# Layer 1 of a two-layer kernel on one core: two batches' gates and shared expert products at a time, the time steps in a lane of their own, and two shared tiles

## Chip, core and metric

The kernel runs on one core of a Trainium2 chip. The metric is the device time of one execution in microseconds (us); it is given as the median of several runs. The engines are TensorE (PE in the profile; PEld is its weight load), VectorE (DVE), ScalarE (ACT), GpSimd (POOL) and SyncE (SP, which here only issues DMAs). Each engine works through its own queue of instructions in order; an instruction that waits holds up all that is queued behind it on the same engine.

## What is computed

The input is x of shape (4, 512, 256): four batches of 512 tokens. Two layers follow, each with a mixer and an expert block. Every block is applied to a layer norm of x, and the layer norm of its result is added to x:

```python
x = x + _layernorm(_L0_attn_ref(_layernorm(x), ...))   # Mamba-like mixer, 32 heads, and a dense feed-forward
x = x + _layernorm(_L0_ffn_ref(_layernorm(x), ...))    # 8 experts, top 2 per token
x = x + _layernorm(_L1_attn_ref(_layernorm(x), ...))   # diagonal state space mixer
x = x + _layernorm(_L1_ffn_ref(_layernorm(x), ...))    # 8 experts, top 2, and a shared expert
```

The change lies in layer 1. Cut to what matters, its two blocks are:

```python
projected = hidden @ in_proj_w.T                          # 256 -> 512 channels
X    = silu(causal_conv(projected))                       # 4 taps along the tokens
gate = sigmoid(hidden @ gate_proj_w.T)
dt   = softplus(einsum('blhp,hp->blh', X, dt_w) + dt_b)   # 8 heads of 64 channels: the time step
a, u = exp(dt * A), dt * B * X
s    = diag_ssm_scan(a, u)                                # s[t] = a[t] * s[t-1] + u[t]
out  = ((C * s + D * X) * gate) @ out_proj_w.T

scores = sigmoid(x @ gate.T)                              # the top 2 of 8 experts keep their score
routed = score of expert e times x                        # for each chosen expert e
out_r  = sum over e of (silu(routed @ w1[e].T) * (routed @ w3[e].T)) @ w2[e].T
out    = (silu(x @ shared_w1.T) * (x @ shared_w3.T)) @ shared_w2.T + out_r
```

## The kernel before

A batch of 512 tokens is the unit of work: x of each batch stays in SBUF as four chunks of 128 tokens, and most tiles are 128 partitions by 512 elements. The first part of the program, up to about 860 us, runs layer 0's mixer for the four batches, with the dense feed-forward of batches 0 to 2 and the routed experts of batches 0 and 1 squeezed in beside it. The second part, which the change touches, has what is left: the dense feed-forward of batch 3 (`last_feed_forward`), the routed experts of layer 0 for batches 2 and 3 (`experts0_in`, `experts0_out`, `experts0_back`), and all of layer 1 for the four batches.

The work of the second part is written as generators, one kind per stage, each run for the batches 0 to 3 in turn. A stage with its place in its list of batches is called a lane. Before the change there are eight lanes: 0 `last_feed_forward`, 1 to 3 the experts of layer 0, 4 `mixer1_in`, 5 `mixer1_out`, 6 `experts1_in`, 7 `experts1_out`. A stage yields after each step a tuple of estimated costs: time on TensorE, time on VectorE, a delay until the next step can start, and at times a fourth number, `need`. A planner at the end of `tile_layers` keeps an estimated clock for TensorE (`pe`) and VectorE (`dve`) and always takes the next step of the lane that is due and stands first in a fixed ranking (batches 2 and 3 before 0 and 1 for the lanes of layer 0 and the mixer). A lane is held back while its `need` names a lane that has not got far enough. The program is then scheduled on the engines' queues by the compiler, which may interleave neighbouring steps further; what counts is the order that comes out on each queue.

What the stages of layer 1 do, with the lines that the profile names:

- `mixer1_in`: layer norm of x (statistics L113 and L114, a power on POOL L123, scaled copies on ScalarE L148), transposes (L135) copied into `xT` by L137; four products with `w1i` (L1054), each followed by the convolution (L199 on ScalarE, three taps L201 on VectorE) and a Silu (L1058) into `X`, which has two buffers; four gate products with `w1g` (L1064) through Tanh (L1065) into `Gt`, one tile of 128 x 4 x 512 with one buffer; then the time steps: 16 small products with `dtw` (L1070), a bias (L1074), a softplus (L206 Abs, L209 Exp, L210 and L211, L212 Ln, L213, L1077). `by_row` turns the steps (L253), copies them (L255) into a tile tagged `row`, writes them to DRAM (L257).
- `mixer1_out`: the steps come back from DRAM, broadcast over 64 partitions (L1088), into `db`, one buffer. For each of four channel blocks: a product on POOL (L1092, `uu`), Exp and a scaled copy on ScalarE (L1093, L1094), on VectorE the scan (L1097), L1098 and the gate (L1099, in place in `Gt`), and four products with `w1o` (L1102). Then add_layernorm (L113, L114, L121, L123, L163, L172).
- `experts1_in`: layer norm, transposes, a bf16 cast (L1136, `xb`), router products (L245), Tanh (L1139), selection of the two experts by small VectorE instructions (L219 to L231, L1142 to L1146), and the shared expert's gated product (L1114, Silu L1116, L1117) into `hs`, one buffer.
- `experts1_out`: for each chunk of 128 tokens two halves of four experts: products (L1164), four Silus (L1169) into a tile tagged `s2b` (two buffers), four VectorE products (L1172) into `he`. For each two chunks: transposes (L1183), copies (L1186, L1188), products (L1194, L1196), add_layernorm, the last scaling on ScalarE (L174) and the store of the result (L1198).

Of the routed experts of layer 0, three lines matter here: the products of a tile of 128 rows (L459 and L467), the gathers of rows and weights by POOL (L441, L444), and, in `experts0_back`, the gathers of the results (L494), which are scaled on ScalarE (L498) and added on VectorE (L499).

ScalarE's functions need tables, and a change from one set to another shows in the profile as an ACT_TABLE_LOAD at the line of the function that needs it.

## Time and profile before

| what | us |
|---|---|
| median of 4 runs | 1298.07 |
| the four runs | 1298.01, 1302.82, 1298.08, 1298.06 |
| the profiled execution, its own time | 1303.1 |
| its span, first to last instruction | 1301.4 |
| PE busy | 1125.3 (86% of the span) |
| DVE busy | 794.5 (61%) |
| ACT busy | 545.1 (42%) |
| POOL busy | 325.0 (25%) |

The profile is of one execution. Its own time is 1.7 us longer than its span, and 5 us longer than the median of the four runs; its mean granted TensorE clock is 0.951. A timeline gives start, duration, engine, line and operation, then in square brackets how long the engine had been idle before and which instruction ended that. A view by stretches of time gives the busy time of each engine in each stretch with the number of its instructions, the granted TensorE clock (1.00 is full speed), the share of the DMA engines and the rate. A view by lines gives for each group of instructions the count, the busy time together, the mean duration in ns of one and the idle time before them. A product of 32-bit numbers shows as two records.

### The profile page before, as it was taken

What the parts mean: (1) busy time and instruction counts of PE and PEld (TensorE: products, weight loads), DVE (VectorE), ACT (ScalarE), POOL (GpSimd) and SP (SyncE); (2) the same over time, 40 slices, a digit from 0 to 9 for tenths busy, and PEclk for the clock granted to TensorE, in tenths of its full rate; (3) what the DMA queues carried; (4) which work ended last, traced back from release to release, by engine and by line L of the source; (5) the groups of instructions that cost most, each with busy time, mean ns of one, the idle gap of its engine ahead of it and who ended that gap; (6) DMA issues with size and microseconds to landing.
All of it is one profiled execution on the core that took longest, in us unless ns stands there. A gap on an engine that the chain in (4) does not pass through costs nothing. (4 is left out here: it accounts for less than half of the span.)

```text
span 1301.4 us, 18525 instructions
## 1 busy us (share of the span) xinstructions
PE 1125.3 (86%) x6896; PEld 698.1 (54%) x6896; DVE 794.5 (61%) x1742; ACT 545.1 (42%) x984; POOL 325.0 (25%) x411
## 2 busy tenths in 40 slices
PE   5688988999888999999989999988988696877876
PEld 3344545556545655555545665554666474454543
DVE  5567766656775564677774556754253554966765
ACT  2253442332434334332424443313154556786644
POOL 4021202001214432111133323123143833120100
PEclk9898999999898999999989999998999898999888
DMA  5010100011104453010114441125365552010100
GB/s 154 19 50 17 33 26 27 17 53 33 33 18 133 153 148 116 25 53 18 50 60 129 151 138 57 46 66 175 101 171 189 162 158 78 1 49 1 42 17 25
DMA packets 76153, 97.41 MB, mean 75 GB/s; under 512 B 11008, under 2 KB 62208, under 8 KB 76064
## 3 DMA queue, kind: packets, MB, share of 16 engines
q0 software_dynamic: 13488, 45.10, 11.8%
q1 hardware_dynamic: 53936, 43.26, 11.1%
q10 hardware_dynamic: 8640, 7.87, 1.8%
q8 instruction: 55, 0.90, 0.3%
q14 instruction: 34, 0.28, 0.1%
HBM read 85.25 MB, written 12.12 MB: 75 GB/s over the span
## 5 line engine op out<-in xcount | busy, mean ns | idle before, releaser
L540 PE MATMUL ps_pj<-uT,wg 128*128 128x512 f32 x512 | 262.2, 637 | 12.6 <-ACT bt L698 7.4
L201 DVE SCALAR_TENSOR_TENSOR BT<-ps_pj,col,BT 128x511 f32<-128x511 f32 (+2 forms) x192 | 143.4, 747 | 120.0 <-ACT BT L199 111.3
L719 POOL TENSOR_SCALAR_AFFINE_SELECT sc<-sc 128x1024 f32<-128x1024 f32 x64 | 69.9, 1092 | 476.0 <-DVE sc L716 468.6
L201 DVE SCALAR_TENSOR_TENSOR CT<-ps_pj,col,CT 128x511 f32<-128x511 f32 (+2 forms) x192 | 142.6, 743 | 21.1 <-ACT CT L199 18.3
L540 PEld LDWEIGHTS ps_pj<-uT,wg 128*128 128x128 f32 x512 | 92.4, 198 | 101.9 <-issue 74.6
L199 ACT ACTIVATE CT<-ps_pj,col 128x512 f32<-128x512 f32 x64 | 49.7, 777 | 119.4 <-PE ps_pj L540 119.4
L713 PE MATMUL ps_dc<-CT,BT 64*128 64x128 f32 x1024 | 89.4, 293 | 7.6 <-DVE sc L716 6.0
L713 PEld LDWEIGHTS ps_dc<-CT,BT 64*128 64x128 f32 x1024 | 70.7, 189 | 46.5 <-issue 29.4
L716 DVE TENSOR_TENSOR sc<-sc,ps_dc 128x1024 f32<-128x1024 f32 x64 | 77.7, 1214 | 23.7 <-PE ps_dc L713 21.2
L308 PE MATMUL ps_dc<-vT,wf 128*128 128x512 f32 x192 | 88.0, 597 | 1.9 <-issue 1.2
L199 ACT ACTIVATE BT<-ps_pj,col 128x512 f32<-128x512 f32 x64 | 49.7, 776 | 85.6 <-PE ps_pj L540 82.0
L708 ACT ACTIVATE sc<-ps_dc 128x1024 f32<-128x1024 f32 x64 | 65.6, 1025 | 40.0 <-PE ps_dc L705 37.6
L444 POOL DMA_INDIRECT wx<-in_w_exp_dram,wrow x60 | 59.2, 986 | 91.2 <-PE ps_dc L467 42.0
L467 PE MATMUL ps_dc<-wx,hx 128*128 128x256 f32 x240 | 65.9, 400 | 10.2 <-ACT h L498 4.7
L459 PEld LDWEIGHTS ps_dc<-hx,wx 128*128 128x128 f32 x480 | 60.9, 191 | 19.4 <-ACT hx L454 9.0
L459 PE MATMUL ps_dc<-hx,wx 128*128 128x128 f32 x480 | 65.1, 279 | 5.0 <-DMA wx<-in_w_exp_dram,wrow 3.0
L441 POOL DMA_INDIRECT xr<-XD,token x60 | 58.7, 979 | 42.2 <-PE ps_dc L452 26.4
L698 ACT COPY bt<-ps_pj 128x384 f32<-128x384 f32 x64 | 30.5, 476 | 82.3 <-PE ps_pj L696 73.3
L463 DVE TENSOR_TENSOR hx<-hx 128x256 f32<-128x256 f32 x60 | 27.5, 459 | 58.6 <-ACT hx L462 43.3
L467 PEld LDWEIGHTS ps_dc<-wx,hx 128*128 128x128 f32 x240 | 43.8, 194 | 29.4 <-issue 8.5
L308 PEld LDWEIGHTS ps_dc<-vT,wf 128*128 128x128 f32 x192 | 35.3, 190 | 42.0 <-issue 39.9
L730 PEld LDWEIGHTS ps_pj<-xd,bt 128*128 128x128 f32 x384 | 47.7, 196 | 16.5 <-issue 8.2
(315 smaller groups left out, 2016.4 us busy)
## 6 DMA issues: line engine op xcount, KB each, us to landing
wg<-in_w_in_dram SPq DMA_DIRECT2D x64, 256.0 KB
YS<-yr ACTq DMA_DIRECT2D x60, 128.0 KB
wf<-in_w_gate_dram SPq DMA_DIRECT2D x32, 128.0 KB
wf<-in_w_up_dram SPq DMA_DIRECT2D x32, 128.0 KB
wf<-in_w_down_dram SPq DMA_DIRECT2D x32, 128.0 KB
db<-dD SPq DMA_DIRECT2D x32, 128.0 KB
St<-Mv SPq DMA_DIRECT2D x192, 2.0 KB
x<-in_x_dram SPq DMA_DIRECT2D x4, 512.0 KB
```

The source lines that it names most:

```text
L199: S.activation(dst, p, AF.Identity, bias=bias, scale=w(3))
L201: V.scalar_tensor_tensor(dst[:, s:], p[:, : L - s], w(3 - s), dst[:, s:], ALU.mult, ALU.add)
L308: T.matmul(p, we[:, i * 2 + k, :], vT[:, k, :], start=(k == 0), stop=(k == 1))
L441: keep(G.indirect_dma_start(out=xr[t], out_offset=None, in_=x, in_offset=bass.IndirectOffsetOnAxis(ap=token[:, t : t + 1], axis=0)))
L444: keep(G.indirect_dma_start(out=ws[t], out_offset=None, in_=w_exp, in_offset=bass.IndirectOffsetOnAxis(ap=wrow[:, t : t + 1], axis=0)))
L459: T.matmul(p[:, L + d * P : L + (d + 1) * P], w[:, k * DM + d * P : k * DM + (d + 1) * P], h[:, k * P : (k + 1) * P], start=(k == 0), stop ...
L467: T.matmul(p[:, 2 * P : 2 * P + DM], h[:, (2 + d) * P : (3 + d) * P], w[:, (2 + d) * DM : (3 + d) * DM], start=(d == 0), stop=(d == 1))
L540: T.matmul(p, w[:, k, :], uT[:, k, :], start=(k == 0), stop=(k == 1))
L708: S.activation(sc, df, AF.Exp)
L713: T.matmul(cb[:, e * L + c * P : e * L + (c + 1) * P], of.BT[e * 64 : (e + 1) * 64, c * P : (c + 1) * P], of.CT[e * 64 : (e + 1) * 64, c * ...
L716: V.tensor_tensor(sc, sc, cb, ALU.mult)
L719: G.affine_select(out=scv, in_=scv, compare_op=ALU.is_ge, fill=0.0, base=0, pattern=[[0, 2 * NC], [1, P]], channel_multiplier=-1)
```

## The change

- `by_row` takes its tile for the turned steps from the tag `s2b`, which the experts' Silus use, with its two buffers; the tag `row` goes.
- The last feed-forward's input `vT` takes the tile `xTe` that `experts1_in` uses for its transposed input, in place of one of its own.
- The tag `hf`, three buffers of 128 x 512 for the last feed-forward's hidden values, gets eight buffers. The gates `Gt` become four tiles of this tag per batch, so that two batches' gates can be held. `hs` gets two buffers.
- `mixer1_in` ends after the gates; the time steps become a stage of their own, `mixer1_steps`, in a lane between `mixer1_in` and `mixer1_out`. There are nine lanes then: 5 is `mixer1_steps`, 6 `mixer1_out`, 7 `experts1_in`, 8 `experts1_out`.
- The planner's holds: before, the gates of batch b waited until `mixer1_out` of batch b - 1 was written out, and the shared product of batch b until `experts1_out` of b - 1 was. Now `X` and the gates of batch b wait for `mixer1_out` of batch b - 2, the gates for the last feed-forward too, and the shared product for `experts1_out` of batch b - 2.
- The planner's estimate for VectorE changes: a step's VectorE time is put after the running VectorE clock or 4 us before the TensorE clock, and no more after the step's own due time.

No arithmetic changes. Lines from L1066 on move by 2, 5 or 10: the gate products become L1066, the step products L1075, the output products L1107, the shared product L1119 and L1122, the expert products L1169, their Silus L1174.

```diff
@@ -251,7 +251,7 @@
         p = ps(bank, 2 if bank == "dc" else 1)
         for c in range(NC):
             T.transpose(p[:8, c * P : (c + 1) * P], wt[:, c, :], ident)
-        wT = wk.tile([8, L], F32, tag="row", name=tag, bufs=1)
+        wT = wk.tile([8, L], F32, tag="s2b", name=tag, bufs=2)
         S.copy(wT, p[:8, :L])
         d = dram.tile([8, L], F32, tag=tag, name=tag, bufs=2)
         nc.sync.dma_start(out=d, in_=wT)
@@ -986,7 +986,7 @@
         wes = [load(f) for f in range(2)]
         yield 0.0, 0.0, 0.0
         v = wl.tile([P, NC, DM], F32, tag="v", name="v", bufs=1)
-        vT = wk.tile([P, 2, L], F32, tag="vTf", name="vT", bufs=1)
+        vT = wk.tile([P, 2, L], F32, tag="xTe", name="vT", bufs=1)
         yield from normed(b, v, vT)
         acc = ps("o", 2)
         pend = []
@@ -1001,7 +1001,7 @@
                 for i, p in enumerate((gp, up)):
                     for k in range(2):
                         T.matmul(p, we[:, i * 2 + k, :], vT[:, k, :], start=(k == 0), stop=(k == 1))
-                h = wk.tile([P, L], F32, tag="hf", name="hf", bufs=3)
+                h = wk.tile([P, L], F32, tag="hf", name="hf", bufs=8)
                 S.activation(h, gp, AF.Tanh, scale=0.5)
                 V.scalar_tensor_tensor(h, h, 1.0, gp, ALU.add, ALU.mult)
                 V.scalar_tensor_tensor(h, h, 0.5, up, ALU.mult, ALU.mult)
@@ -1046,7 +1046,7 @@
         yield 0.0, 2.8, 4.0
         xT = wk.tile([P, 2, L], F32, tag="xTb", name="xT1", bufs=1)
         turned(xT, xn, "b")
-        yield 1.0, 0.0, 1.8
+        yield 1.0, 0.0, 1.8, 18
         t.X = X = wk.tile([P, 4, L], F32, tag="X", name="X", bufs=2)
         for m in range(4):
             p = ps("b")
@@ -1056,14 +1056,19 @@
                     later(i)
             conv(X[:, m, :], p, lambda t, m=m: cv("cw1", m * 4 + t), cv("cb1", m))
             S.activation(X[:, m, :], X[:, m, :], AF.Silu)
-            yield 1.72, 2.3, 0.0, (5 if m == 3 else 0)
-        t.Gt = Gt = wk.tile([P, 4, L], F32, tag="Gt", name="Gt", bufs=1)
+            yield 1.72, 2.3, 0.0, (19 if m == 3 else 0)
+        t.Gt = []
         for m in range(4):
+            g = wk.tile([P, L], F32, tag="hf", name="Gt", bufs=8)
+            t.Gt.append(g)
             p = ps("b")
             for k in range(2):
                 T.matmul(p, w1g[:, k, m * P : (m + 1) * P], xT[:, k, :], start=(k == 0), stop=(k == 1))
-            S.activation(Gt[:, m, :], p, AF.Tanh, scale=0.5)
+            S.activation(g, p, AF.Tanh, scale=0.5)
             yield 1.72, 0.0, 0.0
+
+    def mixer1_steps(b, t):
+        X = t.X
         dp = ps("b").rearrange("p (c a h) -> p c a h", a=16, h=8)
         for c in range(NC):
             for m in range(4):
@@ -1096,10 +1101,10 @@
                 yield 0.0, 0.0, 2.0
             V.tensor_tensor_scan(s, a[:, m, :], s, 0.0, ALU.mult, ALU.add)
             V.scalar_tensor_tensor(s, s, BC[:, m : m + 1], X[:, m, :], ALU.mult, ALU.add)
-            V.scalar_tensor_tensor(Gt[:, m, :], Gt[:, m, :], 1.0, s, ALU.add, ALU.mult)
+            V.scalar_tensor_tensor(Gt[m], Gt[m], 1.0, s, ALU.add, ALU.mult)
             yield 0.0, 2.8, 0.3
             for c in range(NC):
-                T.matmul(outs[:, c * DM : (c + 1) * DM], Gt[:, m, c * P : (c + 1) * P], w1o[:, m, :],
+                T.matmul(outs[:, c * DM : (c + 1) * DM], Gt[m][:, c * P : (c + 1) * P], w1o[:, m, :],
                          start=(m == 0 and c % 2 == 0), stop=(m == 3 and c % 2 == 1), skip_group_check=True)
             yield 1.72, 0.0, 0.0
         yield 0.0, 0.0, 0.5
@@ -1144,8 +1149,8 @@
         V.tensor_tensor(o1, o1, o2, ALU.add)
         t.s = small.tile([P, NC, 8], F32, tag="s1", name="s1")
         V.tensor_tensor(t.s, o1, sc, ALU.mult)
-        yield 1.8, 4.5, 0.5, 7
-        t.hs = wk.tile([P, L], F32, tag="hs", name="hs", bufs=1)
+        yield 1.8, 4.5, 0.5, 28
+        t.hs = wk.tile([P, L], F32, tag="hs", name="hs", bufs=2)
         gated(t.hs, sw1, sw3, xT)
         yield 3.44, 0.7, 0.5
 
@@ -1213,7 +1218,7 @@
     none = lambda b: iter(())
     stages = [lambda b: last if b == B - 1 else none(b)]
     stages += [lambda b, f=f: f(b, held1[b]) if b > 1 else none(b) for f in (experts0_in, experts0_out, experts0_back)]
-    stages += [lambda b, f=f: f(b, held1[b]) for f in (mixer1_in, mixer1_out, experts1_in, experts1_out)]
+    stages += [lambda b, f=f: f(b, held1[b]) for f in (mixer1_in, mixer1_steps, mixer1_out, experts1_in, experts1_out)]
     N = len(stages)
     rank = [2, 3, 0, 1]
     left = [[0.0] * N for _ in range(B)]
@@ -1223,11 +1228,15 @@
     while any(l[0] < B for l in lanes):
         ready = []
         for n, (b, gen, at, need) in enumerate(lanes):
-            if n == 5 and lanes[0][0] < B or need and lanes[need][0] < b:
+            if n == 6 and lanes[0][0] < B:
+                continue
+            if need in (18, 19) and lanes[6][0] < b - 1 or need == 19 and lanes[0][0] < B:
+                continue
+            if need == 28 and lanes[8][0] < b - 1:
                 continue
             if b < B and (gen or n == 0 or lanes[n - 1][0] > b):
                 at = at if gen or n == 0 else max(at if b == 0 else 0.0, left[b][n - 1])
-                first_of = min(rank[b:]) if n < 6 else rank[b]
+                first_of = min(rank[b:]) if n < 7 else rank[b]
                 ready.append((at, (first_of if n < 4 else 4 + first_of) + 0.1 * n, n))
         now = [r for r in ready if r[0] <= pe] or [min(ready)]
         at, _, n = min(now, key=lambda r: r[1])
@@ -1243,8 +1252,9 @@
             pe = max(pe, at) + step[0]
             at = pe
         if step[1]:
-            dve = max(dve, at - step[0]) + step[1]
-            at = max(at, dve if step[2] else dve - 4.0)
+            dve = max(dve, pe - 4.0) + step[1]
+            done = max(dve, at - step[0] + step[1])
+            at = max(at, done if step[2] else done - 4.0)
         l[2] = at + step[2]
         l[3] = step[3] if len(step) > 3 else 0
 
```

## Prediction

> **What bounds the kernel now.** I read the page first, then busy time by stretches of the tail, then VectorE's and TensorE's timelines there. The page: no engine is full, and the chain that ended last is spread thin over all of them, with no single line to remove.
>
> ```profile
> span 1301.4 us, 18525 instructions
> ...
> PE 1125.3 (86%) x6896; PEld 698.1 (54%) x6896; DVE 794.5 (61%) x1742; ACT 545.1 (42%) x984; POOL 325.0 (25%) x411
> ...
> DVE 5%; PE 4%; ACT 4%; issue 2%; POOL 2%; DMA 0%; POOLq 0%; ACTq 0%; SPq 0%; DVEq 0%
> ```
>
> The change touches layer 1 and the last feed-forward alone, so I went to the tail. The last product of layer 0's routed experts (L467, batch 3) starts at 1074.30 and takes 1.13, so it ends at T = 1075.4. After T only layer 1 is left. The stretches (columns as the first line says; counts in brackets) are cut at T and where VectorE starts four marked instructions.
>
> ```profile
> core 0: us, PE busy (x) PEld busy (x) DVE busy (x) ACT busy (x) POOL busy (x), PEclk, DMA share, GB/s
> 1002.00:1075.40 73.40, 57.02 (x283) 42.00 (x284) 38.77 (x97) 40.40 (x83) 41.77 (x38) 0.93 0.55 161
> 1075.40:1100.10 24.70, 15.72 (x85) 11.20 (x84) 8.90 (x32) 16.73 (x29) 10.14 (x10) 0.90 0.30 92
> 1100.10:1150.00 49.90, 40.02 (x182) 23.68 (x182) 39.38 (x115) 38.18 (x72) 7.49 (x7) 0.95 0.01 4
> 1150.00:1206.70 56.70, 45.94 (x198) 28.13 (x197) 39.53 (x107) 39.88 (x74) 9.83 (x7) 0.92 0.08 29
> 1206.70:1256.00 49.30, 38.47 (x208) 25.55 (x207) 37.15 (x114) 27.94 (x62) 8.47 (x8) 0.85 0.11 33
> 1256.00:1301.40 45.40, 31.21 (x166) 17.86 (x164) 24.90 (x100) 17.96 (x53) 2.79 (x4) 0.87 0.07 24
> 1075.40:1301.40 226.00, 171.36 (x833) 106.42 (x831) 149.86 (x463) 140.70 (x287) 38.72 (x36) 0.90 0.09 30
> ```
>
> The reader is to see that after T nobody is full: in 226.0 us TensorE is busy 171.4, VectorE 149.9, ScalarE 140.7. Time is lost in waits between them. The marks in VectorE's timeline are the shared expert's product of batch 0 (L1117) and the casts of batches 1 and 2 (L1136):
>
> ```profile
> 1100.11 0.67 DVE L1117 TENSOR_TENSOR hs<-sg,ps_dc 128x512 f32<-128x512 f32 x1
> ...
> 1150.00 0.69 DVE L1136 CAST xb<-xT 128x1024 bf16<-128x1024 f32 x1 [0.67 <-ACT xT L137]
> ...
> 1206.67 0.69 DVE L1136 CAST xb<-xT 128x1024 bf16<-128x1024 f32 x1 [1.18 <-ACT xT L137]
> ```
>
> TensorE's timeline shows the kind of loss (in brackets: idle before it, and who ended it). These are the three largest single waits after 1101; all its waits after T that the timeline lists add up to 40 us.
>
> ```profile
> 1202.90 1.02 PE L253 MATMUL ps_b<-ident,dts 128*8 128x128 f32 x4 [5.26 <-DVE dts L1077]
> ...
> 1220.18 1.06 PE L1183 MATMUL ps_b<-identb,he 128*128 128x128 bf16 x4 [5.39 <-DVE he L1172]
> ...
> 1250.77 1.95 PE L135 MATMUL ps_dc<-ident,xn 128*128 128x128 f32 x4 [3.00 <-ACT xn L148]
> ```
>
> The first is batch 3's time step: between the Exp and the Ln of its softplus ScalarE loaded tables four times in 5 us (loads of 1.28 at 1197.65, 1199.19, 1200.87, 1202.41), since the experts' Silu stood between. The other two wait for VectorE's expert product and for a layer norm, both queued in order with nothing else ready.
>
> **The change, part by part.** The instruction orders of the two compiled programs hold no times, but say what moves.
>
> *Moved across T.* The count of TensorE's instructions up to the last L467 is nearly the same in both programs, but ahead of T the changed one has also the last two gate products of batch 1 (4 records, 1.7 us from eight in 3.6), its time step product (L1070, 3.7), its transposes (L253, 0.4) and batch 2's input transposes (8 in 1.8): 7.5 us of TensorE. They go into the stretch 1002 to 1075.4, where TensorE's listed waits add up to 16.8 us (the largest, 4.75 before 1015.75, is for ScalarE's scaling of gathered rows). So they need not delay T, but from 1040 on TensorE is over 90% busy, so I let 2 us through: T becomes 1077.4. If nothing were absorbed it is 7.5; if the missing table loads (below) shorten the stretch, it is -3.
>
> *VectorE after T.* I add the rows' busy time per instruction over every VectorE instruction issued after that point (expert product 0.29, convolution tap 0.73, scan 1.27, add of a normed row 0.48, statistics 0.39 and 0.15, and so on). Before: 168.1. After: 171.0, as batch 0's add_layernorm and its next statistics come to stand behind T, and batch 1's first scans go ahead of it. Rows overlap, so 168.1 shows as 149.9 busy; I use the sums on both sides. Before, the five stretches hold 10.6, 43.9, 43.2, 41.4 and 29.0 in 24.7, 49.9, 56.7, 49.3 and 45.4 us: 0.43, 0.88, 0.76, 0.84 and 0.64 of the time. After, the sums are 38.7 up to batch 0's shared expert product, 38.3 up to batch 1's cast, 38.6 up to batch 2's shared product, and 55.4 to the end.
>
> *First stretch after.* In VectorE's new order batch 3's gathered rows, batch 2's convolution, batch 1's last scans and batch 3's norms all stand ahead of batch 2's time step. The gathers:
>
> ```profile
> 1081.09 1.02 POOL L494 DMA_INDIRECT h<-YS,place  x1 [8.91 <-issue]
> ...
> 1090.06 0.96 POOL L494 DMA_INDIRECT yg<-YS,place  x1 [0.30 <-issue]
> ```
>
> They start 5.7 after T and are 1.28 apart, and VectorE takes the last one 17.5 after T (L499 at 1092.88). In POOL's new order they stand behind batch 0's rsqrt and the last product `uu` of batch 1. Those need some 4.7 of VectorE's rows and 1.3 of POOL after T, about 6: hidden behind the 5.7; any delay beyond costs batch 3 one for one. Behind the last gather stand 6 taps (4.4), statistics (2.3), two scans and a product (3.3), a rsqrt on POOL with its hops (1.2), four adds (2.9), statistics (2.3) and three products (2.2): about T+37, with gaps T+38.5. Then the time step's chain: from its bias add to L253 took 7.7 (1080.75 to 1088.41) and 7.8 (1195.07 to 1202.90): T+46.2. On TensorE that wait (L253) now has batch 0's last router products (0.7), batch 3's transposes (1.8) and batch 0's shared expert (3.6) behind it, and then Silu 0.6: batch 0's shared product comes at T+53. TensorE has 33 us of work in it (16 records of L1054 and of L1064 at 0.45 each, 26 of L1102 at 0.22, and the above), so it idles about 20.
>
> TensorE's clock shows what such idling costs: after the 5.39 wait four transposes L1183 took 1.06, where eight usually take 0.61, and the granted clock is 0.85 and 0.87 in the last two stretches. I add nothing, since VectorE ends this stretch. The Trainium skill, "TensorE: Matmul & The Clock Gate", section "Why this matters for your kernels", speaks against this change: no gaps over about 3 us between bursts of matmuls, or the clock falls back to half. By its window of 3.4 us, three such gaps would cost an estimated 3 times 1.7 us, and the sum below would end 5 us later.
>
> *Next stretches.* Batch 2's scans, batch 3's convolution and batch 0's experts are all ready together, as between 1100 and 1150, with the same eleven table loads; at that stretch's 0.88, 38.3 take 43.5. The next 38.6 at the mean of the three middle stretches (128.5 in 155.9, 0.82) take 46.8. Bounds: 0.76 and 0.95.
>
> *Last stretch.* Three batches' experts follow each other, since all four mixers are now done first; batch 3's chain of norm, transposes and router (1238 to 1270 in the open before) is behind batch 1's and 2's products. The last batch alone takes 30.8 (first L1164 of batch 3 at 1270.60 to 1301.4) and holds 16.2 of the sum (32 products 9.3, two copies 1.4, two norms 5.5). The other 39.2 I take at 0.95: one table is loaded in it, against eleven in the stretch at 0.88. Bounds 0.76 and 1.12 (168.1 over 149.9, never waiting). 41.3 + 30.8 = 72.1.
>
> *Table loads.* 56 instead of 63 of ScalarE, five of the seven after T: 7 at 1.28 are 9.0 us of ScalarE. They are in the shares above; for themselves I count nothing, as ScalarE is busy 62% there. Between Exp and Ln of batch 3 no Silu stands any more: the 5.26 wait should be about 2.6 (two loads) shorter.
>
> *Shared tiles.* The row tile that by_row now takes from `s2b` holds one of the two Silu buffers until its DMA has read it. In the new order at least 4.5 us of ScalarE instructions lie between the copy and the next Silu that needs that buffer. The 16 KB store and the broadcast load after it took 7.5 together at worst without other cover (L253 1202.90 to POOL's product at 1210.39), so the store alone is below it: 0, at most 3 for each of batches 2 and 3. The feed-forward's input in `xTe` waits for nobody, since mixer1_out and so experts1_in came after the last feed-forward already. `hf` with 8 and `hs` with 2 buffers add no instruction. On SP's queue all loads of `db` now stand ahead of the output stores; with one buffer they wait, as before, for the last scan of the mixer before.
>
> *Sum.* T 1077.4 + 53 + 43.5 + 46.8 + 72.1 = 1292.8 against 1301.4, so 8.6 less. The profiled execution took 1303.1 (1.7 around its span), the median of the four runs is 1298.07: I take the difference off the median, **1289.5 us**.
>
> **Rivals.**
> 1. *Larger gain.* The new order lets VectorE keep 0.88 all the way to the last 14 us (after batch 3's last expert product, 1287.5, only a tail of 5 is left): (171.0 - 5) / 0.88 + 14 = 203, and T 1077.4: 1280, or with T unmoved 1278, so 21 to 23 less: 1276. For it: 0.88 was reached with eleven loads in it. Against: the first stretch is chained, as worked out.
> 2. *No difference.* The idle time moves: what the last stretch gains, the first one (20 us idle TensorE) gives back. With 0.76 in the two middle stretches they take 101.2 instead of 90.3, and the sum is 1303.7 on the span, or +2: 1300.
> 3. *Slower.* The mechanism is TensorE's queue ahead of T: batch 1's gates and steps stand between batch 3's routed experts, and if the 16.8 us of waits there stay where they are (they end with gathers and ScalarE's queue, which the change does not hurry) the 7.5 us are added to T. Then VectorE at its present mean (168.1 in 226.0, 0.744) takes 171.0 / 0.744 = 230, 4 more: +11, 1309. It decides where T slips by more than 5 and the mean share does not rise.
> 4. *It doesn't do what it says*: ruled out by the order; two batches' gates are issued before the first output product.
>
> **Numbers.** Forecast (its own range 1282 to 1294) 0.44; larger gain 0.16; no difference 0.17; slower 0.23. So faster by over 0.3% (3.9 us, about what a measurement of this kernel can tell from none) 0.60, within it 0.17, slower 0.23. The range reaches from past the larger gain, 1271, to the slower rival, 1309; the middle bound of 0.95 and T at -3 lie inside it.
>
> **What would show it.** T between 1074 and 1080. Batch 0's shared product on VectorE about 53 after T, with TensorE waiting there for the time step. The 5.26 wait at batch 3's L253 about halved. In the last 70 us three batches' L1164 in a row, no wait of 3 us for a layer norm between, VectorE busier than the 24.9 in 45.4 it has now. Wrong it would be if T slips by 6 or more, or if VectorE's share after T stays at 0.66 busy.

## The result, and the profile after

The changed kernel takes 1306.44 us (median of 48 runs, 1298.13 to 1316.69), the kernel before beside it 1300.36 (74 runs, 1294.64 to 1309.37): a ratio of 1.0041, 95% interval 1.0030 to 1.0051. It is slower by 0.4%, where 0.7% faster was forecast. The profiled execution took 1308.19, its span is 1306.5, its mean clock 0.948.

The lines of the page of after that answer to those of before:

```profile
span 1306.5 us, 18519 instructions
...
PE 1129.3 (86%) x6896; PEld 700.3 (54%) x6896; DVE 795.6 (61%) x1742; ACT 536.9 (41%) x977; POOL 322.0 (25%) x411
...
PE 3%; DVE 2%; ACT 1%; issue 0%; POOL 0%; POOLq 0%; ACTq 0%; DVEq 0%
```

Seven instructions of ScalarE are gone (984 to 977), as the orders said: the table loads. TensorE is busy 4 us longer for the same 6896 records.

T, the end of the last L467, is 1087.2 in place of 1075.4 (forecast 1077.4). Below are the stretches of after by time, the first ahead of T, the others cut where the forecast cut them: batch 0's shared product, batch 1's cast, batch 2's shared product, the end.

```profile
core 0: us, PE busy (x) PEld busy (x) DVE busy (x) ACT busy (x) POOL busy (x), PEclk, DMA share, GB/s
1000.00:1087.16 87.16, 65.32 (x327) 48.77 (x326) 39.18 (x82) 45.04 (x94) 39.28 (x38) 0.90 0.49 148
1087.16:1135.77 48.61, 37.79 (x139) 23.26 (x138) 33.53 (x97) 26.83 (x44) 15.95 (x14) 0.86 0.12 37
1135.77:1180.87 45.10, 37.47 (x163) 22.04 (x163) 35.54 (x90) 36.61 (x63) 8.10 (x7) 0.96 0.04 15
1180.87:1222.40 41.53, 29.77 (x148) 19.96 (x146) 32.55 (x107) 24.63 (x45) 8.84 (x8) 0.92 0.12 39
1222.40:1306.50 84.10, 64.36 (x340) 37.17 (x339) 49.03 (x189) 40.55 (x120) 5.18 (x7) 0.84 0.06 20
```

Behind T the forecast was 53, 43.5, 46.8 and 72.1, in all 215.4. Measured: 48.6, 45.1, 41.5 and 84.1, in all 219.3. So two terms failed, T (9.8 us more than forecast) and the last stretch (12.0 more). The first and third stretch came 9.7 shorter together, the second 1.6 longer: 13.7 in all, from 1292.8 to 1306.5.

Where T slipped is seen when both kernels are cut at the first product of batch 0's `mixer1_in` (first w1i product, 959.6 and 961.8) and at T. The views by stretches, before and then after:

```profile
959.60:1075.40 115.80, 95.95 (x503) 70.47 (x502) 57.42 (x157) 61.79 (x125) 55.94 (x53) 0.95 0.53 161
```

```profile
961.80:1087.20 125.40, 102.80 (x536) 76.14 (x536) 57.34 (x140) 64.39 (x132) 51.66 (x51) 0.92 0.50 152
1087.20:1306.50 219.30, 169.34 (x784) 102.40 (x782) 150.61 (x481) 128.62 (x269) 38.07 (x36) 0.88 0.08 26
```

Up to T TensorE has 33 records and 6.9 us more to do, and its idle time has not become less but more, 22.6 in place of 19.9 (125.40 - 102.80, 115.80 - 95.95). On balance no moved work went into a wait. (The other 2.2 of the 11.8 lie ahead of the first w1i product, which came between 938.6 and 968.8 in the executions below, whatever the kernel; all sums from here on start at it.)

The longest waits ahead of T again end with gathered rows (`xr`): 4.06 and 6.81 in after, the second in the line below. The waits of 0.6 us or more up to there add up to 13.0, against 15.3 up to 1030.3 in the kernel before, so they did not grow. The added idle time comes later, in one place that the forecast did not look at. Batch 0's step products are done at 999.5, but its L253 comes only at 1041.83, behind eight input and all eight gate products of batch 1, as the new lane ranks behind `mixer1_in`; before it came at 1004.46. TensorE's timeline, before and then after:

```profile
1004.46 0.60 PE L253 MATMUL ps_b<-ident,dts 128*8 128x128 f32 x4 [1.56 <-DVE dts L1077]
```

```profile
1020.05 0.66 PE L452 MATMUL ps_dc<-ident,xr 128*128 128x128 f32 x2 [6.81 <-DMA xr<-XD,token]
...
1041.83 0.38 PE L253 MATMUL ps_b<-ident,dts 128*8 128x128 f32 x2
```

The broadcast then meets the gathers of the last expert tiles (DMA share 0.83 between 1041.83 and 1055.40). ScalarE's timeline of after:

```profile
1044.58 0.56 ACT L255 COPY dD<-ps_b 8x512 f32<-8x512 f32 x1
...
1057.11 1.28 ACT L1098 ACT_TABLE_LOAD   x1 [5.28 <-DMA db<-dD]
1058.47 0.72 ACT L1098 ACTIVATE db<-db,An 128x512 f32<-128x512 f32 x1
1059.10 0.35 ACT L470 COPY yr<-ps_dc 128x256 f32<-128x256 f32 x1
1059.35 0.39 ACT L462 ACTIVATE hx<-ps_dc 128x256 f32<-128x256 f32 x1
```

and TensorE's:

```profile
1059.79 1.53 PE L467 MATMUL ps_dc<-wx,hx 128*128 128x256 f32 x4 [4.40 <-ACT hx L462]
```

ScalarE stood 5.28 us before the Exp (with its table load in front) until the broadcast landed; the experts' copies `yr` and `hx` were queued behind it, and TensorE waited 4.40 for `hx`.

### The profile page after: what moved, and what is told of

It is laid out like the page before. It is cut to its first block, busy times and chain, and to the rows that moved or that the text cites. A ratio compares the mean times of both kernels' runs of the same rounds, so it can differ in the third digit from the quotient of the medians.

```text
span 1306.5 us, 18519 instructions
## 1 busy us (share of the span) xinstructions
PE 1129.3 (86%) x6896; PEld 700.3 (54%) x6896; DVE 795.6 (61%) x1742; ACT 536.9 (41%) x977; POOL 322.0 (25%) x411
## 5 line engine op out<-in xcount | busy, mean ns | idle before, releaser
L201 DVE SCALAR_TENSOR_TENSOR CT<-ps_pj,col,CT 128x511 f32<-128x511 f32 (+2 forms) x192 | 142.7, 743 | 20.8 <-ACT CT L199 17.9
L540 PEld LDWEIGHTS ps_pj<-uT,wg 128*128 128x128 f32 x512 | 92.7, 199 | 102.2 <-issue 74.6
L708 ACT ACTIVATE sc<-ps_dc 128x1024 f32<-128x1024 f32 x64 | 65.6, 1025 | 39.8 <-PE ps_dc L705 37.8
L444 POOL DMA_INDIRECT wx<-in_w_exp_dram,wrow x60 | 58.5, 976 | 90.4 <-PE ps_dc L467 48.6
L467 PE MATMUL ps_dc<-wx,hx 128*128 128x256 f32 x240 | 64.4, 394 | 9.8 <-ACT hx L462 8.1
L459 PEld LDWEIGHTS ps_dc<-hx,wx 128*128 128x128 f32 x480 | 62.0, 194 | 18.1 <-ACT hx L454 9.0
L459 PE MATMUL ps_dc<-hx,wx 128*128 128x128 f32 x480 | 66.1, 281 | 2.3 <-ACT hx L454 1.9
L467 PEld LDWEIGHTS ps_dc<-wx,hx 128*128 128x128 f32 x240 | 43.3, 191 | 28.2 <-ACT hx L462 14.4
```

What stands on the lines that cost most here:

```text
L201: V.scalar_tensor_tensor(dst[:, s:], p[:, : L - s], w(3 - s), dst[:, s:], ALU.mult, ALU.add)
L444: keep(G.indirect_dma_start(out=ws[t], out_offset=None, in_=w_exp, in_offset=bass.IndirectOffsetOnAxis(ap=wrow[:, t : t + 1], axis=0)))
L459: T.matmul(p[:, L + d * P : L + (d + 1) * P], w[:, k * DM + d * P : k * DM + (d + 1) * P], h[:, k * P : (k + 1) * P], start=(k == 0), stop ...
L467: T.matmul(p[:, 2 * P : 2 * P + DM], h[:, (2 + d) * P : (3 + d) * P], w[:, (2 + d) * DM : (3 + d) * DM], start=(d == 0), stop=(d == 1))
L540: T.matmul(p, w[:, k, :], uT[:, k, :], start=(k == 0), stop=(k == 1))
L708: S.activation(sc, df, AF.Exp)
```

## The experiments

Three theories on where the time went. **A, late steps:** the slip of T comes from the late L253 and from instructions on ScalarE that wait for a DMA ahead of the experts' copies. **B, moved work:** the work ahead of T is simply added to it. **C, the estimate:** the planner's new estimate for VectorE puts the wrong work ahead. And for the last stretch: either VectorE paces it, as the forecast had it, or TensorE with its clock, or the chain through each chunk.

All runs in one table: the ratio to the kernel before, run on the same chip; the time from the first w1i product to T, with TensorE's busy and idle time in it; the time from T to the end; and their sum.

| kernel | ratio (95%) | to T (busy, idle) | T to end | sum |
|---|---|---|---|---|
| before | 1 | 115.8 (96.0, 19.9) | 226.0 | 341.8 |
| after | 1.0041 (1.0030 to 1.0051) | 125.4 (102.8, 22.6) | 219.3 | 344.7 |
| e1 steps first | 0.9976 (0.9950 to 1.0001) | 120.0 (100.6, 19.4) | 218.1 | 338.1 |
| e2 hold gates | 0.9993 (0.9974 to 1.0012) | 113.4 (95.8, 17.7) | 224.5 | 337.9 |
| e3 both | 0.9960 (0.9938 to 0.9982) | 120.6 (100.7, 19.9) | 215.0 | 335.6 |
| e4 old estimate | 0.9979 (0.9952 to 1.0005) | 133.9 (113.0, 20.9) | 207.1 | 341.0 |
| e5 load later | 0.9957 (0.9935 to 0.9979) | 118.8 (99.8, 19.0) | 212.9 | 331.7 |
| e6 before, new estimate | 0.9998 (0.9976 to 1.0020) | 108.8 (91.6, 17.2) | 233.0 | 341.8 |
| e7 before, shared tiles | 1.0014 (0.9987 to 1.0042) | 118.6 (100.9, 17.7) | 224.8 | 343.4 |
| e8 e3 and gap 1.9 | 0.9879 (0.9841 to 0.9917) | 118.2 (100.4, 17.8) | 209.7 | 327.9 |
| e9 after again | 1.0012 (0.9990 to 1.0033) | 122.7 (101.8, 20.9) | 219.9 | 342.6 |
| e10 after, 16 and 1.9 | 0.9982 (0.9958 to 1.0007) | 116.5 (98.2, 18.3) | 218.2 | 334.7 |
| e11 before, gap 1.9 | 0.9990 (0.9971 to 1.0009) | 116.1 (96.6, 19.5) | 225.7 | 341.8 |
| e12 more VectorE | 1.0033 (1.0007 to 1.0059) | 122.9 (102.3, 20.6) | 219.5 | 342.4 |
| e13 more TensorE | 1.0015 (0.9983 to 1.0047) | 124.2 (101.6, 22.6) | 214.2 | 338.4 |
| e14 before, estimate, gap | 1.0015 (0.9984 to 1.0045) | 115.4 (94.0, 21.4) | 226.4 | 341.8 |
| e15 e8 again | 0.9888 (0.9839 to 0.9937) | 118.2 (100.3, 17.9) | 209.8 | 328.0 |
| e16 e8, filled | 0.9924 (0.9898 to 0.9950) | 117.8 (100.9, 16.9) | 212.9 | 330.7 |
| e17 after, half filled | 0.9979 (0.9959 to 0.9999) | 124.6 (102.2, 22.4) | 213.6 | 338.2 |

A ratio's interval is some 0.2 to 0.5% wide to each side; the sums of the same kernel agree within 2.1 (after and e9) and 0.1 (e8 and e15). The sums come from one execution each, the ratios from many: where they differ, the ratio is the verdict and the sum tells the place.

**e1, steps first.** The lane of the steps goes ahead of `mixer1_in`:

```diff
-                ready.append((at, (first_of if n < 4 else 4 + first_of) + 0.1 * n, n))
+                ready.append((at, (first_of if n < 4 else 4 + first_of) + (0.35 if n == 5 else 0.1 * n), n))
```

> The changed kernel, with the lane of the time steps ranked ahead of the lane of mixer1_in (everything else as changed; in TensorE's order batch 0's L253 moves from behind batch 1's input and gate products to directly behind its own step products). Theory A, late steps: the last L467 ends at 1087.2 instead of 1075.4 because batch 0's L253 came at 1041.8 instead of 1004.5, its broadcast landed only at 1057.2 on busy DMA engines, and ScalarE stood 5.28 us before the Exp with the copies of batch 3's expert tiles (hx) behind it in its queue. By A the last L467 ends at 1074 to 1080, no L467 waits over 2 us for hx, and the whole takes 6 to 11 us less than the changed kernel, about 1295 to 1300. Theory B, moved work: the 7.5 us of TensorE work that stand ahead of the last L467 are simply added to it. By B the last L467 stays at 1083 or later and the time within 3 us of the changed kernel, 1304 to 1309.

The ratio is 0.65% below that of after, as A had it, but T was not: 120.0 from the first w1i product, where 1074 to 1080 mean 112 to 118. The wait at batch 0's first Exp is gone; an 8.70 wait of L459 for `hx` stands at 997 instead (ScalarE waits there before L498 for gathered rows), and one of 2.85 of L467 for `hx` at 1061, behind batch 1's first Exp. TensorE's busy time stays 4.7 above before. Half of A and a good part of B.

**e2, gates held.**

```diff
-            if need in (18, 19) and lanes[6][0] < b - 1 or need == 19 and lanes[0][0] < B:
+            if need == 18 and lanes[6][0] < b - 1 or need == 19 and (lanes[6][0] < b or lanes[0][0] < B):
```

> The changed kernel, with the gates of batch b held again until mixer1_out of batch b - 1 is written out, as before (time steps still in their lane of their own, behind mixer1_in). In TensorE's order batch 0's output products come earlier, ahead of batch 1's last gates, and batch 1's gates and steps go back behind or to the last of the expert tiles. Theory A, late steps: batch 0's L253 now follows batch 1's input products and not its gates, so it comes at about 1025 instead of 1042, and the wait for the broadcast falls on other work: the last L467 ends at 1076 to 1081. The part after it loses what two batches' gates gave, 219.3 goes back to about 226: in all 1300 to 1307. Theory B, moved work: the last L467 ends at 1075 to 1078 as in the kernel before, and the whole takes what the kernel before takes, within 3 us.

With the gates back behind T, T comes 113.4 after the first w1i product, busy 95.8: what B says. The part behind goes back to 224.5, as both expected. The ratio, 0.9993, is that of the kernel before.

**e3, both.**

> The changed kernel with both: the lane of the time steps ranked ahead of mixer1_in, and the gates of batch b held until mixer1_out of batch b - 1 is written out. Ahead of the last L467 its order is close to the kernel before. Theory A (late steps) and theory B (moved work) both expect the last L467 at 1074 to 1078. What comes after it tells what two batches' gates are worth there: if the 6.7 us gained after the last L467 by the change (226.0 to 219.3) come from the gates, it takes 224 to 228 here and the whole is within 4 us of the kernel before; if they come from other parts (the planner's estimate, the shared product's two buffers), it takes 217 to 222 and the whole is 4 to 9 us below the kernel before.

T did not come at 1074 to 1078 (112 to 116 from the first w1i product, counted as for e1) but at 120.6: the order is not as close to before as I took it to be, batch 1's steps still stand ahead. T to end is 215.0, better than with two batches' gates ahead (219.3): the gain behind T doesn't need them.

**e4, the old estimate.** The last part of the diff undone:

```diff
-            dve = max(dve, pe - 4.0) + step[1]
-            done = max(dve, at - step[0] + step[1])
-            at = max(at, done if step[2] else done - 4.0)
+            dve = max(dve, at - step[0]) + step[1]
+            at = max(at, dve if step[2] else dve - 4.0)
```

> The changed kernel with the planner's old estimate for VectorE's time (the last part of the change undone alone). In TensorE's order batch 0's L253 stands early again, ahead of batch 1's input products, while batch 2's first eleven input products also go ahead of the last L467 (about 5 us more of TensorE work than in the changed kernel). Theory A, late steps: no wait over 2 us of L467 for hx; the last L467 ends 2 to 8 us earlier than the changed kernel's 1087.2 in spite of more work ahead of it, 1079 to 1085. Theory B, moved work: it ends later than in the changed kernel, at 1090 or above. For the whole, A expects 1298 to 1305, B 1304 to 1312.

17 us more of TensorE's work than in before stand ahead of T (113.0 busy), T is later by 18 and the rest shorter by 19, the idle time ahead of T as large as ever. By T that is B; the whole, 0.9979, lies at the low end of A's. Moving work across T gives nothing and takes nothing here; what counts is the sum.

**e5, load later.** One number of the changed kernel:

```diff
         t.dD = by_row(dts, "b", "dD")
-        yield 0.5, 0.0, 9.0
+        yield 0.5, 0.0, 16.0
```

> The changed kernel with one number altered: the planner's delay between the step's transposes (L253) and mixer1_out is 16 us in place of 9, about what the write and the broadcast took (L255 at 1044.6, broadcast landed at 1057.2, 12.6). Batch 0's Exp then stands some three expert tiles later in ScalarE's queue; batch 0's steps stay as late as in the changed kernel. Theory A, an instruction that waits for a DMA holds up the experts' copies behind it on ScalarE: no L467 waits over 2 us for hx behind the first Exp, and from the last L1054 of batch 0's successor, that is from batch 0's L253 to the last L467, it takes 38 to 42 us in place of 45.3 (1041.8 to 1087.2). Theory B, moved work: with 8 output products fewer ahead of it the same stretch is 2 us shorter and no more, 43 or above. What mixer1_out loses by coming later comes behind: the whole within 5 us of the changed kernel by both.

From L253 to T it takes 38.7, inside A's bounds, but not for A's reason alone: ScalarE still stood 4.15 us before the Exp, and TensorE waited 2.43 and 2.10 for `yr`, in place of 4.40 and 2.11 for `hx`. Of the 6.6 us, 3.7 are TensorE's work that now comes behind T (36.2 busy to 32.5) and 2.9 are idle time (9.1 to 6.2). The whole fell by 0.8%, more than either theory gave.

**e6 and e7, one part alone on the kernel before:** the planner's estimate (the diff of e4, the other way round), and the two shared tiles (the first two parts of the change).

> The kernel before with the last part of the change alone, the planner's estimate for VectorE's time. Theory A, late steps: the estimate did no harm by itself, since batch 0's steps stay directly behind their products here; from the first w1i product to the last L467 112 to 118 us (115.8 in the kernel before), and a ratio to the kernel before of 0.996 to 1.001. Theory C, the estimate puts the wrong work ahead: 1.003 or above, with the loss ahead of the last L467. That undoing the estimate in the changed kernel gave 0.9979 in place of 1.0041 speaks for C so far.

> The kernel before with the shared tiles alone: the turned time steps in the Silus' tag, the feed-forward's input in xTe. Forecast 0, at most 3 us each for batches 2 and 3. Expected: a ratio of 0.998 to 1.002, and no wait over 1 us of ScalarE's Silu L1116 or of the turned steps' copy L255 that the DMA to DRAM ends. If the shared tile is part of the loss, it shows as 1.003 or above.

Neither alone moves the time beyond its interval. The estimate moves 4.4 us of TensorE's work behind T and leaves the sum at 341.8, so C falls as a cause by itself. Together with the rest of the change it stays open: e4, which undoes the estimate there, has a ratio 0.6% below that of after and 0.3% below that of e9. The tiles: no loss that can be told from none.

**e8, e10, e11, e14, e15, the gap.** One number, in e3's kernel (e8, e15), in after together with e5's number (e10), in before (e11), in before with the new estimate (e14):

```diff
-    def experts0_back(b, t, gap=1.0):
+    def experts0_back(b, t, gap=1.9):
```

> The kernel of e3_steps_first_hold (0.996) with one number more: the planner's gap between the steps in which experts0_back gathers, scales and adds a chunk is 1.9 us in place of 1.0, so the first scaling (L498) stands further behind in ScalarE's queue. In e3 TensorE waited 8.28 us at 994 for hx (L454), because ScalarE stood before L498 until its gathered rows came. Theory A in its general form (any instruction on ScalarE that waits for a DMA holds up the experts' copies): that wait falls below 4 us, and the whole takes 3 to 6 us less than e3, a ratio of 0.991 to 0.994. Rival: the wait only moves to the next gather (xr behind the gathers of the results on POOL, at least 1.25 us each), and the whole stays within 2 us of e3, 0.9945 to 0.998.

> The changed kernel with two numbers of the planner altered and nothing else: the delay between L253 and mixer1_out 16 us in place of 9 (as in e5_load_later, 0.9957), and the gap of experts0_back 1.9 us in place of 1.0 (as in e8_first_hold_gap). Theory A in its general form: each takes an instruction that waits for a DMA out of the way of the experts' copies on ScalarE; the two add up, to a ratio of 0.988 to 0.993. Rival: the change's own order (batch 1's gates ahead, steps late) costs several us besides, so the ratio stays at 0.994 or above.

> The kernel before with the gap of experts0_back at 1.9 us alone. It tells whether the 0.988 of e8_first_hold_gap belongs to the change with its two holds, or to this number. In the kernel before TensorE waited 4.75 us at 1015.75 behind the same scaling L498, and 2.82 behind hx. Theory A: about half of these go, 2 to 5 us, a ratio of 0.996 to 0.999; the rest of e8's gain, 0.7% or more, then is the change's. Rival: the number alone gives what e8 has, 0.990 or below.

> The kernel before with the planner's new estimate and the gap of 1.9 us, without the lane, the gates, the buffers and the shared tiles. If the gain of e8_first_hold_gap (0.988) comes from the estimate together with the gap, this has 0.986 to 0.992. If the gates of two batches, the shared product's second buffer and the lane are needed for it, it has 0.996 to 1.002, as each of the two alone (0.9998 and 0.999).

> The kernel of e8_first_hold_gap unaltered, for a comparison with e14 on one chip: the lane of the steps ranked ahead of mixer1_in, gates held one batch, gap 1.9. By what e8 showed a ratio of 0.984 to 0.992; where the gain were that chip's own, 0.994 or above.

e8 and e15 are the fastest here, 1.2% and 1.1% below before: the version that beats both. The reason A gave is not it. The wait for L454 fell from 8.28 to 5.11 and another of 5.00 for L255 came beside it; ahead of T only 2.4 us were won, and 5.3 behind T. On before the same number gives nothing (e11, e14), and in e10 it adds nothing to e5's. So it is the order that comes out of rank, hold and gap together. What that order has less of is long waits of TensorE behind T: three of 2.9 us or more in e8 and in e15 (5.0, 5.0 and 3.0), against five in before, in after and in e3, and six in e9. Which of the moved steps brings that is open.

**e9, after once more.**

> The changed kernel once more, unaltered, for a trace beside the next ones. A ratio to the kernel before of 1.002 to 1.006, and between the transposes of batch 0's steps (L253) and the last L467 again 43 to 47 us with a wait of L467 for hx of 3 to 5 us at the first Exp. If the 0.41% came from a chance placing of DMA traffic in one execution, the wait is gone here or the ratio lies at 1.000 or below.

42.9 us from L253 to T, at the low edge of what was expected, and the wait at the first Exp again, shorter (2.93, this time for `yr`): no chance of one execution. The ratio of 1.0012 doesn't tell a loss from none by itself; the set of 48 runs does. The two intervals only just meet (at 1.0030 to 1.0033), so the size of the loss is less sure than either says.

**e12, more work for VectorE.** Behind each half chunk's `he` of batches 2 and 3 a product that nobody uses:

```diff
+                if b > 1:
+                    V.tensor_tensor(extra, he[:, half * 4 : half * 4 + 4, :].rearrange('p e t -> p (e t)'), w1i[:, 1, :], ALU.mult)
```

> The changed kernel with 16 more products of 128x512 on VectorE whose result nobody uses, one behind each half chunk's he in the routed experts of batches 2 and 3 of layer 1: 8 per batch, about 0.7 us each by the product into hs (L1122, 0.69), 11 us in all, in the last 84 us. The forecast took VectorE as what sets the pace there, at 0.95 of the time; it came to 84.1 where 72.1 was forecast. If VectorE does set the pace, all of it shows: 10 to 12 us more than the changed kernel, a ratio of 1.012 to 1.014. If the pace is set by the chain of each chunk through TensorE, ScalarE and VectorE, or by TensorE (64.4 of 84.1 busy), less than half shows: 0 to 5 us, a ratio of 1.004 to 1.008.

The last stretch, from batch 2's shared product on, in e9 and then in e12:

```profile
1228.00:1311.40 83.40, 63.68 (x340) 36.95 (x339) 48.81 (x188) 40.45 (x119) 5.19 (x7) 0.85 0.06 20
```

```profile
1221.90:1305.60 83.70, 61.31 (x340) 35.94 (x339) 58.42 (x205) 40.86 (x119) 5.19 (x7) 0.85 0.06 20
```

VectorE has 9.6 us more to do and the stretch is 0.3 longer; the whole is 2.4 longer by the medians on the same chip (1308.46 and 1306.10). VectorE does not pace the stretch.

**e13, e17, e16, more work for TensorE.** Behind the same half chunks 64 (e13) or 32 (e17) products that nobody uses, in the changed kernel; 64 in e8's (e16):

```diff
+                if b > 1:
+                    for i in range(4):
+                        T.matmul(extra[0], xb[:, 0, c * P : (c + 1) * P], fw1[:, half * 4 : half * 4 + 4, 0, :], start=True, stop=True)
```

> The changed kernel with 64 more products of 128x512 bf16 on TensorE whose result nobody uses, four behind each half chunk of the routed experts of batches 2 and 3 of layer 1: 0.26 us each by the rows of four (L1169, 1.02), 16 us of TensorE in the last 84 us (TensorE busy 64.4, granted clock 0.84). If TensorE paces that stretch, all of it shows: 13 to 17 us more. If the latency of each chunk's chain does (product, Silu, he, transposes, copy, products, statistics), the products fall into TensorE's waits: 0 to 6 us more. If a lower clock after waits is what makes it long, the waits filled raise the granted clock there from 0.84 to 0.90 or more, and the other products' busy time falls.

> The changed kernel with 32 unused products, two behind each half chunk of batches 2 and 3, in place of e13's 64. If the clock's fall after waits sets the length, the last stretch (from batch 2's hs L1122 to the end: 83.4 to 84.1 without, 78.7 with 64) lies between, 79 to 83, with a granted clock between 0.85 and 0.94. If there is a threshold, it is at one of the two ends.

> The kernel of e8_first_hold_gap (0.988, the last L467 to the end 209.7) with the 64 unused products of e13 behind the half chunks of batches 2 and 3. If the clock's fall after waits is the cause, the part behind the last L467 becomes shorter here too, by 1 to 4 us (its last 78 us have a granted clock of 0.90, less to gain than at 0.84), 206 to 209. If e13's gain was that order's own, 16 us of products cost some of their time in a part that is better filled: 212 or more.

More work makes the stretch shorter: 78.7 with 64 products, 78.1 with 32, against 83.4 to 84.1. In e13 and then in e17:

```profile
1205.40:1284.10 78.70, 65.96 (x402) 38.34 (x400) 48.47 (x188) 40.19 (x119) 5.18 (x7) 0.94 0.06 21
```

```profile
1220.10:1298.20 78.10, 60.91 (x371) 35.28 (x369) 48.83 (x189) 40.24 (x119) 5.19 (x7) 0.95 0.06 21
```

Batch 3's shared product cuts the stretch in two at the same point of the work. The views, in after and then in e17, show the first 12 us and the two parts (the clock is the third number from the end; batch 2's shared product starts at 1222.58 in after, 0.2 behind the cut used so far):

```profile
1222.40:1234.40 12.00, 9.93 (x36) 5.24 (x36) 5.34 (x22) 7.38 (x20) 1.01 (x1) 0.58 0.01 1
1222.58:1254.91 32.33, 27.54 (x144) 16.04 (x144) 20.30 (x84) 16.71 (x48) 2.40 (x3) 0.84 0.03 10
1254.91:1306.50 51.59, 36.83 (x196) 21.14 (x195) 28.56 (x105) 23.66 (x72) 2.78 (x4) 0.83 0.08 26
```

```profile
1220.10:1232.10 12.00, 10.57 (x68) 6.41 (x67) 6.56 (x28) 7.81 (x21) 1.01 (x1) 1.00 0.00 1
1220.18:1250.51 30.33, 27.38 (x166) 15.94 (x165) 20.21 (x85) 16.45 (x48) 2.40 (x3) 1.00 0.03 10
1250.51:1298.20 47.69, 33.45 (x206) 19.34 (x204) 28.55 (x105) 23.71 (x72) 2.79 (x4) 0.92 0.08 28
```

In after TensorE had waited for batch 2's shared product just before; in e17 the unused products ended that wait earlier:

```profile
1223.30 1.02 PE L1169 MATMUL ps_dc<-fw,xb 128*128 128x512 bf16 x4 [3.59 <-DVE hs L1122]
```

```profile
1219.58 1.67 PE L1183 MATMUL ps_o<-fw,xb 128*128 128x512 bf16 x7 [2.28 <-DVE x L172]
```

Behind the wait of 3.59 the granted clock is 0.58 for 12 us and TensorE finishes 36 records; behind the one of 2.28 it is 1.00 and TensorE finishes 68, 15 of them unused. Over the stretch one product of L1169 takes 426 ns in after, 397 in e17 and 379 in e13.

That wait is not the whole gain. The part that holds it, up to batch 3's shared product, is 2.0 us shorter in e17 than in after (33.4 in e9, 30.8 in e13); the part behind it is 3.9 shorter (50.1 in e9, 48.0 in e13). There the clock of after falls to 0.50 too, behind shorter waits (the first row of the second view is the one behind 3.59):

```profile
1267.99 1.06 PE L1188 MATMUL ps_b<-identb,he 128*128 128x128 bf16 x4 [1.54 <-DVE he L1177]
...
1277.60 0.75 PE L1188 MATMUL ps_b<-identb,he 128*128 128x128 bf16 x3 [2.42 <-DVE he L1177]
```

```profile
1224.23:1234.47 10.24, 9.06 (x33) 4.91 (x32) 3.51 (x15) 7.11 (x18) 1.01 (x1) 0.50 0.01 2
1268.60:1272.01 3.41, 3.38 (x14) 1.93 (x14) 1.40 (x6) 0.92 (x2) 0.00 (x0) 0.50 0.23 77
1278.84:1282.25 3.41, 3.41 (x16) 1.63 (x13) 1.50 (x6) 1.17 (x5) 0.00 (x0) 0.50 0.23 77
```

In e9, on the other hand, a wait of 3.92 left it at 1.00 for the next 12 us:

```profile
1113.30 3.67 PE L1066 MATMUL ps_b<-xT,w1g 128*128 128x512 f32 x8 [3.92 <-DVE X L201]
```

```profile
1113.30:1125.30 12.00, 10.34 (x44) 6.15 (x45) 10.27 (x33) 5.44 (x10) 2.42 (x2) 1.00 0.01 1
```

So the length of a single wait does not tell which clock follows. What the two fills show is that more work in TensorE's idle time raised the clock over the stretch from 0.84 to 0.95 (e13: 0.94) and made it 5 to 6 us shorter; no run holds the clock fixed, so that the clock does it is the reading that fits.

In e8's kernel, whose last 78 us had 0.90 granted, the fill costs 3.2 us behind T (209.7 to 212.9). That is what was expected where the gain belongs to the order of after and not to filling as such. e17's ratio, 0.9979, is below both of after's (1.0041 and 1.0012); e13's, 1.0015, doesn't tell.

## Why the prediction was wrong, point by point

- **T slips by 2.** Wrong by 9.8. The step that failed is "they need not delay T": I set 7.5 us of moved work against 16.8 us of waits. Of the work 5.8 to 6.9 showed as busy time of TensorE and none went into a wait; the idle time ahead of T is 16.9 to 22.6 in all 19 traces, whatever stands beside it. The waits end with gathers and with ScalarE's queue, and the moved products stand in TensorE's order where they were due, not where it waits. That is the mechanism of rival 3. The rest, 1.1 to 2.8 of idle time, is the late L253 and the Exp on ScalarE, which no rival had: I checked the queue behind the moved wait on TensorE, and not what stood behind the Exp on ScalarE.
- **First stretch 53.** It was 48.6. The chain was right: the gathers start 7.0 behind T (5.7 said), the last row is taken at 19.2 (17.5), L253 of batch 2 comes at 42.4 (46.2). But TensorE waited there only 0.84, and idles 10.8 in the stretch instead of 20, as it is busy 37.8 at a granted clock of 0.86 where I counted 33.
- **Middle stretches 43.5 and 46.8.** 45.1 and 41.5, VectorE's sums at 0.85 and 0.93, inside the bounds of 0.76 and 0.95.
- **Last stretch 72.1.** Wrong by 12.0, and this alone turns the sign: with it right, and the rest as measured, the sum would be 1294.5, below the span before of 1301.4. (T alone would do it too, at 1296.7.) The step is "the other 39.2 I take at 0.95". VectorE was busy 49.0 of 84.1, and e12 shows that it doesn't pace the stretch. TensorE has 64.4 in it: 72.1 would have needed 0.89 of its time, more than it has in any stretch behind T, before or after. One batch at a time leaves TensorE to wait for each link, at a granted clock of 0.84. Filling these waits takes off 5 to 6 us (e13, e17). The other 6 I put down to the chain through each chunk, as what is left; no run took it away, so this is argued and not shown.
- **The clock rule.** The rows say that behind the 3.59 wait the clock is 0.58 for 12 us, and behind 2.28 it is 1.00. The Trainium skill, "TensorE: Matmul & The Clock Gate", section "Why this matters for your kernels", asks for no idle gaps over about 3 us, and these two rows agree. Others of this case are not told by it: 0.50 behind waits of 1.54 and 2.42, and 1.00 behind 3.92 in e9. I had weighed three such gaps for the first stretch, at 5 us, and added nothing. That filling the last stretch gave 5 to 6 us is near that figure by luck: it did not come by three such gaps.
- **Wait of 5.26 at batch 3's L253 halved.** It is 1.34, and the seven table loads are gone.
- **Shared tiles 0.** Held: e7 1.0014, interval 0.9987 to 1.0042.
- **VectorE's share** behind T rose from 0.663 (149.9 of 226.0) to 0.687 (150.6 of 219.3), so rival 3, right on T, was wrong on the rest: it had 230 behind T. What came is rival 3's T and, behind it, 6.7 of the 10.6 us that were forecast.
- **Slips in the working.** TensorE's terms named for the first stretch add up to 26.2 (14.4 + 5.7 + 6.1), not 33; the steps behind the last gather to T+36.1, not 37; TensorE's listed waits after T to 46.0, not 40; and between 1100 and 1150 ScalarE loaded tables ten times, not eleven. None of them turns the sign.

The change gains 6.7 behind T and loses 9.6 ahead of it. Most of both is the same work on the other side of the mark: over the sum TensorE is idle 72.6 in place of 74.5, and busy 272.1 in place of 267.3 at a lower clock (e9: 73.8 and 268.8). So what is missing of the expected gain lies mainly in the last stretch, three batches in a row that no other work fills, at a granted clock of 0.84.

## What to carry to other kernels

A wait on a bottleneck's timeline is room for other work only if that work stands, in that engine's order, right behind the wait: look where it will be queued before setting it against the waits. When work is pulled ahead, ask what is left for the end: a last stretch with one item in flight leaves every engine waiting (here TensorE busy 64.4 and VectorE 49.0 of 84.1 us), so sum every engine's work in it and not only that of the one you think paces it. And look at the granted clock of a stretch in which TensorE often idles: here 32 unused products took 5 to 6 us off 84 us at 0.84, while 64 of them cost 3.2 where it was 0.90 already.

## What the runs showed of the hardware

- 32 products of no use made a stretch of 84 us 5 to 6 us shorter, with 0.95 of the clock granted in place of 0.84; where the clock was granted at 0.90 already, 64 of them cost 3.2.
- The clock fell to 0.50 behind single waits of TensorE of 1.54, 2.42 and 3.59 us, and stayed at 1.00 behind one of 2.28 and one of 3.92.
- The part ahead of the first w1i product came to 938.6 to 968.8 us in the traces, while the part behind it agreed within 0.1 us for e8 and e15 and within 2.1 for after and e9. For a change in the second part the sum from that mark tells the place of a difference that the whole time hides.
- The eight loads of 128 KB of one batch's broadcast (L1093) took SP's queue 8.1 us among the gathers, with the DMA engines at 0.83, and the last had landed 12.5 us after the copy L255 began; in the kernel before they took it 5.1 (L1088).
